# Graph attention with two GCN layers: most of the projections moved from ahead of the attention into it, and value weights of 9 columns instead of 32

## The chip, the cores and the metric

The kernel runs on one core of one Trainium2 chip. The metric is the device time of one execution in microseconds (us), the median of the runs given. PE is TensorE (matmuls), ACT is ScalarE, DVE is VectorE, POOL is GpSimd, and SP is SyncE, which issues all transfers of this kernel.

## What is computed

```python
# _layernorm: (y - mean) / sqrt(var + 1e-5) over the last axis
# N = 2708 nodes, D = 128 features, H = 8 heads; adj is 2708 x 2708, fp32
q = (x @ Wq.T).reshape(d, n, h)      # d = 128, n = 2708, h = 8
k = (x @ Wk.T).reshape(d, n, h)
v = (x @ Wv.T).reshape(d, n, h)
a = einsum('dnh,dmh->dnm', q, k) * d ** -0.5
a = softmax(a + adj + adj, axis=2)
o = einsum('dnm,dmh->dnh', a, v).reshape(n, h * d)
x = _layernorm(x + o @ Wo.T)
# second layer
h1 = adj @ (x @ W2) + b2
x = _layernorm(x + adj @ (h1 @ W4) + b4 + h1 @ res_w.T + res_b)
```

The reshape makes 128 attention batches of 2708 queries and keys with only 8 features each. One batch takes 2708 x 8 consecutive numbers of the projected rows, that is about 21 tokens of 1024 projected values.

## The kernel before

**Projections.** The first block (L300 to L349) projects all tokens: 22 chunks of up to 128 tokens (`MC`), each with the three weights. A projection is two matmuls of 128x512 into the tile `pp` (L317). For q and k, ACT writes the value rounded to the format fp32r (L326), DVE writes what the rounding left (L327) and the largest absolute value (L334, into `ends`), and SP stores both parts to DRAM (`qs`, L329; `ks`, L332). For v, ACT copies (L321) and SP stores (`vs`, L322). Amid the last chunks SP loads the keys, queries and values of the first group and the first adjacency columns. Then POOL reorders keys (`order_keys`, L252 and L256) and spreads values (`spread_values`, L268).

**Attention.** Four batches make a group (`GB`), so there are 32 groups. The queries of a group are taken in 6 blocks of 452 or 448 columns (`QBS`), the keys in 21 chunks of 128 and one of 20. A block is worked in 9 steps (`plan`), so there are 1728 steps. A step has two to four pieces and one chunk on the side (`TWO_EXP`):

- a piece is two score matmuls into one of two PSUM tiles `s` (`score`, L374), and one DVE addition of the adjacency columns to both (`add_near`, L381), into the tile `e`, of which there are four;
- the chunk on the side has three score matmuls into the PSUM tile `p`, an exponential by ACT (L456) and a product with exp of the adjacency by POOL (L457), tile `w`;
- at the end of the step one exponential by ACT (L459) over all pieces.

The matmuls of values (`add_up`, L395) sum a chunk into `acc`: four matmuls, one for each batch, each on its own 32 of the 128 output partitions. The weight of each is `v[:, m, ds(VW * j, VW)]` with `VW = 32` columns: 8 of the batch's values and 24 of ones, the first of which sums the weights. A block ends with a copy by DVE (`hand_on`, L401) and four stores (L403). In the first group ACT also makes the exponentials of the adjacency (`first_exp`, L362).

**Order.** From L407 on the order is the program's (`manual_schedule`). The generator `interleave` (L39) writes it: it keeps a model of when PE, ACT, DVE and POOL come free, with a constant for each kind of work, and picks at each point the next piece or the next `add_up` that is ready. SP's loads are put at the first piece of a step: `load_adj` keeps 8 loads ahead (`ahead`), `load_q`, `load_keys` and `load_values` are spread over a block or a group.

**The rest.** `layer0_out` divides, multiplies with Wo and normalizes; `layer1` does the two products with the adjacency. A fallback, `attention_with_maxima`, is only run where the numbers are out of range.

Of the kernel before, what the change touches and what calls it, by code (L numbers as in the profile page):

```python
# [9 lines left out]
F32 = mybir.dt.float32  # L10
F32R = mybir.dt.float32r
I32 = mybir.dt.int32
AF = mybir.ActivationFunctionType
ALU = mybir.AluOpType
AX = mybir.AxisListType
# [8 lines left out]
VW = 32  # L24
# [14 lines left out]
def interleave(plan, blocks, short, bufs=4, patience=0.1):  # L39
# [8 lines left out]
    EXP, EXP_ADDED, EXP_TILE = 0.07, 0.14, 0.37  # L48
    n_plan = len(plan)
# [12 lines left out]
    n, c, left = 0, 0, None  # L62
    while n < blocks * n_plan or queue:
        starts = []
        if n < blocks * n_plan:
# [29 lines left out]
        again = False  # L95

# [33 lines left out]
def graph_attention_gcn(ctx: ExitStack, tc: tile.TileContext, x, xT, adj, adjT, adjP, adjS,  # L130
# [35 lines left out]
    qs = dram.tile([N, 2 * H, P], F32, name="qs")  # L166
# [6 lines left out]
    ends = const.tile([P, 2, NM], F32, name="ends")  # L173
# [3 lines left out]
    with ExitStack() as s:  # L177
# [10 lines left out]
        v_short = [kept.tile([P, GB * VW], F32, name=f"v_short{i}") for i in range(2)]  # L188
        vals = [kept.tile([P, NU, GB * VW], F32, name=f"vals{i}") for i in range(2)]
        for t in k_short:  # L190
            nc.gpsimd.memset(t.bitcast(F32), 0.0)
        for t in v_short:
            nc.gpsimd.memset(t, 0.0)
            for j in range(GB):
                nc.gpsimd.memset(t[ds(32 * j, SHORT), ds(VW * j, VW)], 1.0)
        for t in vals:
            nc.gpsimd.memset(t, 1.0)
# [36 lines left out]
        def whole_tokens(r0, n):  # L234

            return ds(r0 // P, (r0 % P + n - 1) // P + 1), r0 % P

# [9 lines left out]
        def order_keys(g, i):  # L247

            t, (k, kz, _, _) = raw_keys[g], groups[g]
            if i < 8:  # L250
                n = P // 8
                nc.gpsimd.tensor_copy(k[:, :, ts(i, n)], t[:, ts(i, n * NU)].rearrange("p (q c) -> p c q", c=NU))  # L252
            else:
                for j in range(GB):
                    r = ds(32 * j, 32)
                    nc.gpsimd.tensor_copy(kz[r, ds(32 * j, SHORT)], t[r, ds(P * NU, SHORT)])  # L256

        def load_values(g, j):
# [5 lines left out]
            nc.sync.dma_start(vz[ds(32 * j, SHORT), ds(VW * j, H)], vs[ds(r0 + P * NU, SHORT), :])  # L264

        def spread_values(g, j):
            to = vals[g % 2].rearrange("p c (j e) -> p j c e", e=VW)
            nc.gpsimd.tensor_copy(to[:, j, :, :H], values[g][:, j, :].rearrange("p (c e) -> p c e", e=H))  # L268

        def load_q(g, b, js=range(GB)):  # L270

            n0, nw = QBS[b]
            if js[0] == 0:
                queries[g, b] = qpool.tile([P, P + (QB + 2 * P - 1) // P * P], F32R, tag="q", name="q")
            for j in js:
                tokens, off = whole_tokens((GB * g + j) * N + n0, nw)
                n = tokens.size
                for i in range(2):
                    to = queries[g, b][ds(32 * j + 2 * H * i, 2 * H), ds(P - off, n * P)].bitcast(F32)
                    nc.sync.dma_start(to.rearrange("p (t g) -> p t g", g=P), qs[tokens].rearrange("t r g -> r t g"))  # L280
# [17 lines left out]


        with ExitStack() as t:  # L300
            wpool = t.enter_context(tc.tile_pool(name="wqkv", bufs=1))
            sb = t.enter_context(tc.tile_pool(name="proj", bufs=4))
            ps = t.enter_context(tc.tile_pool(name="ps_proj", bufs=4, space=PSUM))

            xT_sb = wpool.tile([P, N], F32, name="xT_sb")
            nc.sync.dma_start(xT_sb[:, :P], xT[:, :P])
            w_sb = []
            for name, w in (("k", WkT), ("q", WqT), ("v", WvT)):
                w_sb.append(wpool.tile([P, H * P], F32, name=f"w{name}_sb"))
                nc.sync.dma_start(w_sb[-1], w)  # L310
            nc.sync.dma_start(xT_sb[:, P:], xT[:, P:])
            v3 = vs.rearrange("(i g) e -> i (g e)", g=P)
            for c, (i0, mi) in enumerate(MC):
                for w, dst in zip(w_sb, (ks, qs, vs)):
                    pp = ps.tile([P, 2, 512], F32, tag="pp", name="pp")
                    for h in range(2):
                        nc.tensor.matmul(pp[:mi, h, :], xT_sb[:, ds(i0, mi)], w[:, ts(h, 512)], start=True, stop=True)  # L317
                    flat = pp[:mi].rearrange("p a b -> p (a b)")
                    if dst is vs:
                        o = sb.tile([P, H * P], F32, tag="po", name="po")  # L320
                        nc.scalar.copy(o[:mi], flat)  # L321
                        nc.sync.dma_start(v3[ds(i0, mi)], o[:mi])  # L322
                    else:
                        f = half_scale if dst is qs else 1.0
                        o = sb.tile([P, 2, H * P], F32R, tag="pr", name="pr")
                        nc.scalar.mul(o[:mi, 0], flat, f)  # L326
                        nc.vector.scalar_tensor_tensor(o[:mi, 1], flat, f, o[:mi, 0].bitcast(F32), ALU.mult, ALU.subtract)  # L327
                        if dst is qs:
                            nc.sync.dma_start(dst.rearrange("i r g -> i (r g)")[ds(i0, mi)],  # L329
                                              o[:mi].bitcast(F32).rearrange("p l f -> p (l f)"))  # L330
                        else:
                            nc.sync.dma_start(dst.rearrange("r (i g) -> i r g", g=P)[ds(i0, mi)],  # L332
                                              o[:mi].bitcast(F32).rearrange("p l (e g) -> p (l e) g", g=P))
                        nc.vector.tensor_reduce(ends[:mi, int(dst is qs), c : c + 1], o[:mi, 0].bitcast(F32), AX.X,  # L334
                                                ALU.max, apply_absolute_value=True)

                if 2 <= c < 10:
                    load_keys(0, 2 * (c - 2))
                    load_keys(0, 2 * (c - 2) + 1)
                elif 10 <= c < 10 + GB:  # L340
                    load_q(0, 0, [c - 10])
                    load_values(0, c - 10)
                elif 10 + GB <= c < 10 + GB + ahead // 2:
                    load_adj(2 * (c - 10 - GB))
                    load_adj(2 * (c - 10 - GB) + 1)
            for h in range(9):
                order_keys(0, h)
            for j in range(GB):
                spread_values(0, j)  # L349

        epool = s.enter_context(tc.tile_pool(name="weights", bufs=4))
        ppool = s.enter_context(tc.tile_pool(name="products", bufs=4))
        opool = s.enter_context(tc.tile_pool(name="sums", bufs=2))
        ps = s.enter_context(tc.tile_pool(name="ps_s", bufs=2, space=PSUM))
        pq = s.enter_context(tc.tile_pool(name="ps_q", bufs=1, space=PSUM))
        pa = s.enter_context(tc.tile_pool(name="ps_a", bufs=1, space=PSUM))

# [8 lines left out]
        def score(to, g, b, m, j):  # L366
            nw = QBS[b][1]
            k, kz, _, _ = groups[g]
            q = queries[g, b][:, ds(P, nw)]
# [411 lines left out]
```

## Time and profile before

| | |
|---|---|
| median of 3 runs | 6965.26 us (6964.58 to 6968.61) |
| the profiled execution | 6968.86 us |
| its span, first to last instruction | 6967.0 us |
| mean granted PE clock | 0.994 |
| busy: PE, DVE, ACT, POOL | 97%, 88%, 94%, 81% |
| first exponential of a step (L459) starts at | 191.09 us |
| exponential of the last step ends at | 6625.1 us |
| DMA | 1654.83 MB, mean 238 GB/s |

The time of an execution is about 1.9 us longer than its span. PE's matmuls are pipelined and their ends are modelled, so PE's busy share says less than the distances from start to start. A share over the whole span mixes the projections, the attention and the rest; the stages are read one by one.

### The profile page before, as it was taken

The page shows a single profiled execution, that of the slowest core. Times are in us where ns is not written, and L with a number is a line of the kernel's source. Part 1 is how long each engine was busy: PE and PEld are TensorE (multiplying, and loading weights), DVE is VectorE, ACT ScalarE, POOL GpSimd, SP SyncE. Part 2 cuts the span into 40 slices and gives each one's busy share as a digit, 9 for nine tenths or more (in the row PEclk, how much of TensorE's full clock was granted, in tenths as well). Part 3 has the DMA queues.
Part 4 walks back from the last instruction along what each step waited for, and adds up shares of the span by engine and source line. Part 5 has one row for each costly group of instructions (what it writes and reads, how often), then busy time and mean ns, then how long its engine had stood idle before and what let it go on. Part 6 is the DMA issues. An engine that isn't in the chain of part 4 may idle for free.

```text
span 6967.0 us, 136616 instructions
## 1 busy us (share of the span) xinstructions
PE 6761.2 (97%) x50426; PEld 2168.4 (31%) x50426; DVE 6098.5 (88%) x6160; ACT 6541.9 (94%) x3659; POOL 5620.3 (81%) x2266
## 2 busy tenths in 40 slices
PE   7899999999999999999999999999999999999979
PEld 2223333333333333333333333333333333333354
DVE  5789999999999999999999999999999999999941
ACT  3999999999999999999999999999999999999920
POOL 0688888888888888888888888888888888888800
PEclk9999999999999999999999999999999999999999
DMA  9887777777777777777777777777777777777667
GB/s 340 264 247 230 235 236 243 230 233 240 234 239 228 234 244 241 229 230 237 239 239 228 234 242 241 231 227 236 238 242 229 233 243 236 235 228 237 219 199 232
DMA packets 1163854, 1654.83 MB, mean 238 GB/s; under 512 B 144372, under 2 KB 1125944, under 8 KB 1156244
## 3 DMA queue, kind: packets, MB, share of 16 engines
q1 hardware_dynamic: 1163176, 1646.00, 76.0%
q8 instruction: 399, 6.54, 0.4%
q14 instruction: 279, 2.29, 0.1%
HBM read 1563.63 MB, written 81.80 MB: 236 GB/s over the span
## 4 chain that ended last, share of the span: by engine, by line
PE 58%; ACT 12%; DVE 9%; DMA 8%; issue 7%; POOL 4%; SPq 2%; DVEq 0%; ACTq 0%; POOLq 0%
PE acc L395 29%; PE s L374 20%; DVE e L381 9%; ACT e L459 7%; ACT w L456 4%; POOL w L457 3%; PE acc L604 3%; DMA col<-in_adjP 3%; PE p L374 2%; PE acc L391 2%; DMA ecol<-ne 2%; DMA qs<-pr 1%; DMA two<-in_adjP 1%; PE s L371 1%; SPq L280 1%
## 5 line engine op out<-in xcount | busy, mean ns | idle before, releaser
L457 POOL TENSOR_TENSOR w<-w,ecol 128x1356 f32<-128x1356 f32 (+1 forms) x1728 | 5353.9, 3104 | 889.2 <-ACT w L456 731.0
L381 DVE TENSOR_TENSOR e<-s,col 128x904 f32<-128x904 f32 (+1 forms) x4608 | 4828.9, 1092 | 396.8 <-PE s L374 147.1
L459 ACT ACTIVATE e<-e 128x2712 f32<-128x2712 f32 (+5 forms) x1728 | 4729.6, 2737 | 0.8 <-DVE e L381 0.8
L395 PE MATMUL acc<-e,vals 128*32 128x452 f32 x21888 | 3812.7, 555 | 11.0 <-ACT e L459 0.5
L374 PE MATMUL s<-q,k 32*128 32x452 f32 x10944 | 2455.5, 465 | 94.7 <-DVE e L381 22.3
L456 ACT ACTIVATE w<-p 128x1356 f32<-128x1356 f32 (+1 forms) x1728 | 2417.4, 1399 | 16.0 <-DMA two<-in_adjP 13.0
L374 PEld LDWEIGHTS s<-q,k 32*128 32x128 f32 x10944 | 1023.2, 181 | 3233.4 <-DVE e L381 2737.2
L395 PE MATMUL acc<-w,vals 128*32 128x452 f32 x10368 | 1652.3, 553 | 0.0
L374 PE MATMUL p<-q,k 32*128 32x452 f32 (+1 forms) x5184 | 1261.9, 438 | 13.9 <-ACT w L456 13.6
L381 DVE TENSOR_TENSOR e<-s,two 128x904 f32<-128x904 f32 (+1 forms) x960 | 1048.4, 1092 | 160.3 <-ACT w L456 98.0
L395 PEld LDWEIGHTS acc<-e,vals 128*32 128x32 f32 x21888 | 619.3, 108 | 849.2 <-issue 781.0
L374 PEld LDWEIGHTS p<-q,k 32*128 32x128 f32 x5184 | 516.7, 182 | 37.7 <-ACT w L456 36.4
L395 PEld LDWEIGHTS acc<-w,vals 128*32 128x32 f32 x10368 | 279.1, 108 | 202.8 <-issue 178.5
L252 POOL CAST k<-k_raw 128x336 fp32r<-128x336 f32 x256 | 226.0, 884 | 16.3 <-DMA k_raw<-ks 16.3
L391 PE MATMUL acc<-e,v_short 128*128 128x452 f32 (+1 forms) x384 | 196.7, 594 | 0.0
L401 DVE COPY o<-acc 128x452 f32<-128x452 f32 x192 | 118.6, 618 | 6.2 <-PE acc L395 6.2
L326 ACT ACTIVATE pr<-pp 128x1024 fp32r<-128x1024 f32 (+1 forms) x44 | 45.1, 1024 | 79.7 <-DMA ks<-pr 44.4
L327 DVE SCALAR_TENSOR_TENSOR pr<-pp,pr 128x1024 fp32r<-128x1024 f32 (+1 forms) x44 | 53.8, 1223 | 75.3 <-ACT pr L326 70.5
L604 PE MATMUL acc<-col,xw 128*128 128x512 f32 (+2 forms) x264 | 106.0, 551 | 0.0
L496 ACT ACTIVATE sd<-mv,eps 128x1 f32<-128x1 f32 (+1 forms) x22 | 5.9, 291 | 104.7 <-DVE mv L490 104.7
L604 PE MATMUL acc<-col,hw 128*128 128x512 f32 (+2 forms) x264 | 104.1, 545 | 0.0
L616 ACT COPY hw<-ph 128x128 f32<-128x128 f32 (+1 forms) x22 | 5.4, 266 | 98.7 <-PE ph L615 98.6
(77 smaller groups left out, 979.9 us busy)
## 6 DMA issues: line engine op xcount, KB each, us to landing
col<-in_adjP SPq DMA_DIRECT2D x1965, 226.0 KB
two<-in_adjP SPq DMA_DIRECT2D x1440, 226.0 KB
ecol<-ne SPq DMA_DIRECT2D x1395, 226.0 KB
col<-in_adjP SPq DMA_DIRECT2D x393, 224.0 KB
two<-in_adjP SPq DMA_DIRECT2D x288, 224.0 KB
ecol<-ne SPq DMA_DIRECT2D x279, 224.0 KB
col<-in_adjT SPq DMA_DIRECT2D x210, 256.0 KB
k_raw<-ks SPq DMA_DIRECT2D x512, 84.6 KB
```

Source lines behind the costliest of these rows:

```text
L252: nc.gpsimd.tensor_copy(k[:, :, ts(i, n)], t[:, ts(i, n * NU)].rearrange("p (q c) -> p c q", c=NU))
L280: nc.sync.dma_start(to.rearrange("p (t g) -> p t g", g=P), qs[tokens].rearrange("t r g -> r t g"))
L371: nc.tensor.matmul(to[:, :nw], kz, q, start=True, stop=True)
L374: nc.tensor.matmul(to[:, :nw], k[r, m, :], q[r], start=True, stop=True)
L381: nc.vector.tensor_add(e[:, ds(at, 2), :nw], st[:, :, :nw], a)
L391: nc.tensor.matmul(a[:, :nw], vz, e[:, t, :nw], start=False, stop=False)
L395: nc.tensor.matmul(a[ds(32 * j, VW), :nw], v[:, m, ds(VW * j, VW)], e[:, t, :nw], start=(m == first_chunk), stop=(m == last_chunk))
L401: nc.vector.tensor_copy(o[:, :nw], acc.pop((g, b))[:, :nw])
L456: nc.scalar.activation(w[:, :, :nw], sp[:, :, :nw], AF.Exp, scale=2.0)
L457: nc.gpsimd.tensor_mul(w[:, :, :nw], w[:, :, :nw], exp_cols[g, b, two][:, :nw].unsqueeze(1).to_broadcast([P, 3, nw]))
L459: nc.scalar.activation(e[:, :at, :nw], e[:, :at, :nw], AF.Exp, scale=2.0)
L604: nc.tensor.matmul(acc[:, :nw], src[:mw, m, :], t[:mw, :nw], start=(m == 0), stop=(last is None and m == NM - 1))
```

## The change

The projections of the first two chunks of tokens (`FIRST = 2`, 256 tokens, enough for the first three groups) stay ahead of the attention, and the pools that only they used are gone: they borrow the tiles `w`, `e` and `s`. The reordering of the first group's keys is shared out to POOL, DVE and ACT. The other 20 chunks are projected half a projection at a time: 120 halves, each one matmul 128x512 into a tile `s`. The planner puts one ahead of steps 2, 8, ... 50, and then one ahead of every 13th step from 56 to 1486. DVE alone does the work after the matmul: three operations for q and k, one copy for v. SP loads the half's weight again (256 KB) right after the half before, and stores the result at the second piece of the following step.

The values of a batch take 9 columns (`VW = H + 1`) instead of 32. The first chunk of a block, which starts the sum, still uses 32, from a small tile `v_first` of its own, that `spread_values` also fills. `qs` is laid out as `ks` is, by feature row, so that a query load takes 16 rows of up to 1808 bytes each.

```diff
-VW = 32
+VW = H + 1
...
-def interleave(plan, blocks, short, bufs=4, patience=0.1):
+def interleave(plan, blocks, short, amid=(), bufs=4, patience=0.1):
...
+    PROJECT, SPLIT = 0.95, 1.75
...
-        if n < blocks * n_plan:
+        if n in amid and c == 0 and seen < n:
+            starts.append((added[-2] + HOP, "amid"))
+        elif n < blocks * n_plan:
...
+        if what == "amid":
+            pe += PROJECT
+            added.append(max(added[-1], pe + SHOWN) + SPLIT)
+            seen = n
+            yield "amid", n, None, None
+            continue
...
-    qs = dram.tile([N, 2 * H, P], F32, name="qs")
+    qs = dram.tile([2 * H, R], F32, name="qs")
...
-            nc.gpsimd.tensor_copy(to[:, j, :, :H], values[g][:, j, :].rearrange("p (c e) -> p c e", e=H))
+            v = values[g][:, j, :].rearrange("p (c e) -> p c e", e=H)
+            nc.gpsimd.tensor_copy(to[:, j, :, :H], v)
+            nc.gpsimd.tensor_copy(v_first[g % 2][:, ds(32 * j, H)], v[:, first_chunk, :])
...
+            q = queries[g, b] = qpool.tile([P, QB], F32R, tag="q", name="q")
+            for j in range(GB):
                 for i in range(2):
...
+                    nc.sync.dma_start(q[ds(32 * j + 2 * H * i, 2 * H), :nw].bitcast(F32),
+                                      qs[:, ds((GB * g + j) * N + n0, nw)])
...
+        proj = s.enter_context(tc.tile_pool(name="proj", bufs=2))
...
+        def split(o, src, i, end, mul=nc.vector.tensor_scalar_mul):
+
+            f = half_scale if i == 1 else 1.0
+            mul(o[:, 0].bitcast(F32R), src, f)
+            nc.vector.scalar_tensor_tensor(o[:, 1].bitcast(F32R), src, f, o[:, 0], ALU.mult, ALU.subtract)
+            nc.vector.tensor_reduce(end, o[:, 0], AX.X, ALU.max, apply_absolute_value=True)
+
+        def load_half(n):
+            c, i, h = halves[n]
+            i0, mi = MC[c]
+            if i == h == 0:
+                given[c] = proj.tile([P, P], F32, tag="xc", name="xc")
+                nc.sync.dma_start(given[c][:, :mi], xT[:, ds(i0, mi)])
+            given[c, i, h] = proj.tile([P, NB], F32, tag="wc", name="wc")
+            nc.sync.dma_start(given[c, i, h], projections[i][0][:, ts(h, NB)])
+
+        def project(n):
+
+            c, i, h = halves[n]
+            i0, mi = MC[c]
+            dst = projections[i][1]
+            pp = ps.tile([P, 2, NB], F32, tag="s", name="s")
+            nc.tensor.matmul(pp[:mi, 0, :], given[c][:, :mi], given.pop((c, i, h)), start=True, stop=True)
+            o = proj.tile([P, 2, NB], F32, tag="pr", name="pr")
+            if i == 2:
+                nc.vector.tensor_copy(o[:mi, 0], pp[:mi, 0])
+                return lambda: nc.sync.dma_start(dst.rearrange("(i g) e -> i (g e)", g=P)[ds(i0, mi), ts(h, NB)], o[:mi, 0])
+            split(o[:mi], pp[:mi, 0], i, ends[:mi, i, ds(2 * c + h, 1)])
+
+            def store():
+                for l in range(2):
+                    nc.sync.dma_start(dst.rearrange("r (i g) -> i r g", g=P)[ds(i0, mi), ds(H * l + 4 * h, 4)],
+                                      o[:mi, l].rearrange("p (e g) -> p e g", g=P))
+            return store
...
+        for n in range(ahead):
+            load_adj(n)
+        load_half(0)
+        for i, (_, dst) in enumerate(projections):
+            for c in range(FIRST):
+                pp = ps.tile([P, 2, NB], F32, tag="s", name="s")
+                for h in range(2):
+                    nc.tensor.matmul(pp[:, h, :], first_x[:, ts(c, P)], first_w[:, ts(2 * i + h, NB)], start=True, stop=True)
...
+            if i == 1:
+                for h in range(16):
+                    load_keys(0, h)
+                load_q(0, 0)
...
+        for h in range(9):
+            order_keys(0, h, (nc.gpsimd.tensor_copy, nc.vector.tensor_copy, nc.scalar.copy)[h % 3])
...
-                nc.tensor.matmul(a[ds(32 * j, VW), :nw], v[:, m, ds(VW * j, VW)], e[:, t, :nw],
-                                 start=(m == first_chunk), stop=(m == last_chunk))
+                if m == first_chunk:
+                    nc.tensor.matmul(a[ds(32 * j, 32), :nw], v_first[g % 2][:, ds(32 * j, 32)], e[:, t, :nw],
+                                     start=True, stop=False)
+                else:
+                    nc.tensor.matmul(a[ds(32 * j, VW), :nw], v[:, m, ds(VW * j, VW)], e[:, t, :nw],
+                                     start=False, stop=(m == last_chunk))
...
+        amid = list(range(2, 54, 6))
+        amid += range(56, 56 + 13 * (len(halves) - len(amid)), 13)
...
+            if what == "amid":
+                at = amid.index(n)
+                stores.append(project(at))
+                if at + 1 < len(halves):
+                    load_half(at + 1)
+                continue
...
+            if c == 1 and stores:
+                stores.pop()()
```

## The prediction

> **What bounds the kernel now.** I read the stages first: the busy time by stretches, whose columns are the stretch, then busy us and instructions of each engine, the clock granted to PE, the DMA share and GB/s.
>
> ```profile
> 0.00:187.00 187.00, 129.49 (x270) 49.41 (x270) 103.08 (x89) 68.88 (x68) 15.57 (x37) 0.92 1.01 336
> 187.00:225.00 38.00, 34.44 (x211) 10.93 (x215) 31.75 (x31) 34.52 (x25) 24.81 (x8) 0.83 0.83 254
> 1000.00:6000.00 5000.00, 4932.57 (x38212) 1515.39 (x38204) 4591.92 (x4496) 4999.40 (x2698) 4378.53 (x1749) 1.00 0.76 236
> 6600.00:6967.00 367.00, 322.00 (x1418) 181.43 (x1410) 129.34 (x333) 65.80 (x96) 22.51 (x13) 0.96 0.68 212
> ```
>
> The first stage is all 22 chunks of projections: the DMA share is 1.01 and no compute engine is full, so transfers end it. The middle stage is another regime: ACT is busy 4999.4 of 5000 us. The next view, ACT's timeline (start, duration), tells whether that is work or stretched waiting.
>
> ```profile
> 2011.54 1.38 ACT L456 ACTIVATE w<-p 128x1344 f32<-128x1344 f32 x1
> 2012.73 3.27 ACT L459 ACTIVATE e<-e 128x3584 f32<-128x3584 f32 x1
> 2015.81 1.37 ACT L456 ACTIVATE w<-p 128x1344 f32<-128x1344 f32 x1
> ```
>
> 1344 elements take 1.19 us from start to start, 3584 take 3.08: the difference is 0.84 ns an element, the same everywhere. ACT works without a pause; only fewer elements could shorten this stage, and the change leaves ACT's exponentials alone. ACT's waits from 225 to 6600 us say the same:
>
> ```profile
> ACT w L456 <- PE p L374: 1.2, 3, 0.6
> ACT w L456 <- PE s L374: 0.4, 1, 0.4
> ```
>
> But the reserve behind it is small. I took, from the timeline of DVE and ACT, the lead with which the last addition (L381) of a step ends before the step's exponential (L459) starts. It is the same in nearly every block of nine steps (step 0 to 8): 0.32, 2.01, 0.67, 1.19, 1.21, 0.33, 0.86, 0.20, 1.11 us. 0.20 is the least ever seen, so at step 7 ACT is just waiting, and from 0 and 5 it is 0.1 away. That wait is hidden in the overlap of two activations, and shows only in start-to-start: 65 ns more at step 6's end and 14 ns at step 7 than elsewhere, 0.08 us a block.
>
> PE's timeline shows its spacing (all from one stretch):
>
> ```profile
> 2010.04 0.96 PE L395 MATMUL acc<-e,vals 128*32 128x448 f32 x8
> 2010.93 0.47 PE L374 MATMUL s<-q,k 32*128 32x448 f32 x2
> 2011.34 0.56 PE L395 MATMUL acc<-e,vals 128*32 128x448 f32 x1
> 2011.74 0.54 PE L395 MATMUL acc<-e,vals 128*32 128x448 f32 x1
> 2012.23 0.82 PE L374 MATMUL s<-q,k 32*128 32x448 f32 x4
> ```
>
> Four batches' value products run side by side, in two passes: 11.34, 11.74, next work at 12.23. PE goes from cluster to cluster with few gaps: against the usual minimum of each kind of transition I find some 225 us of slack in 5000, 1.5 us a block of 33.4.
>
> **What the Trainium skill says.** "TensorE: Matmul & The Clock Gate", section "LDWEIGHTS": a load's time goes with the number of columns, P/1.2 ns, not with rows. The trace agrees: at 452 columns pass to pass is 403 ns, 27 above the 376 that the shortest transitions take, and 32/1.2 is 27. By the same page 9 columns cost 7.5 ns (an estimate; the trace has no such load). "ScalarE: Activation LUTs", section "What ACT_TABLE_LOAD costs": 0.833 ns an element; the trace's 0.84 agrees. "VectorE: DVE Perf Modes", section "Mode 1× (REGULAR)": fp32 and PSUM operands fall back to one element a cycle, at 0.96 GHz; the 904 elements of L381 in 1.09 us agree.
>
> **The change, part by part.** *Start.* In before the first exponential of a step (L459) starts at 191.09 us. After, the chain is: wk in at 5.3 (as now); k for two chunks through PE, ACT (1.02) and DVE (1.22 + 1.21 each): stores of ks at 11 and 14; q follows as banks come free: stores at 16 and 18. The queue ahead of them holds 1.7 MB of x and weights, 2.5 MB of adjacency, 0.3 MB of the next half; with the four 1 MB stores 8.5 MB, at 336 GB/s 25 us, so q has landed at about 28. SP issues 16 key loads and 8 query loads at 0.4 us from 19 on: landed at about 35. Then 9 key reorderings on three engines (POOL 0.88 each): 38. Queries land meanwhile. Four additions of 1.0 us: **first exponential at 44 us** (36 if the transfers overlap better, 55 if each hop waits for its store; the value stores and loads come after, and are needed a step or two later). Removed: 191 − 44 = **147 us** (136 to 155).
>
> *Nine value columns.* 20 of the 21 chunks (the first stays 32 wide) save 27 − 7.5 ns ahead of both passes, 0.04 us a chunk, 0.78 us of PE a block. On ACT's path that is worth only the 0.08 us a block that it waits now: 192 × 0.08 = 15, I take **−10 us**. Its use is slack.
>
> *Projections amid.* 120 halves: 9 in the first 54 steps, then 111, one every 13 steps (48 us) up to step 1486. Each has a 128x512 matmul, 2 × 0.43 (the spacing of L317) plus a load: 0.95 us of PE; at 0.69 a block this is 0.66 us, less than the 0.78 gained, and within the slack of 1.5 anyhow. A k or q half (80 of them) gives DVE three operations of 512 elements, (1.22 − 0.53) − 0.08 overlap = 0.6 us each: 1.8 us. A v half gives 0.6. DVE's own work is 29 additions at 1.01 and one copy, 29.8 of 33.4 us; 1.0 more fits on average. On ACT: nothing. What counts is the moment: DVE is 1.8 us late at once, and ACT's lead is 0.1 to 1.8 above its minimum. I walked the nine steps (13 steps apart, the halves fall on each in turn): DVE's pauses beyond back-to-back, that can be used to catch up, are 0.28, 0.66, 0.56, 0, 0.49, 0.37, 0.65, 0.25, 0.35 us in steps 0 to 8. Late time less pauses less lead is what ACT loses: inserted ahead of step 0 to 8 1.4, 0.1, 0.8, 0.8, 0.8, 1.3, 0.9, 1.6, 1.1, mean 0.97. The shorter loads raise the leads by some 85 ns a step (2.2 chunks × 0.04), 0.2 until the weak step comes: 0.75 us. 73 such halves: **+55**. For 38 v halves the rule gives 0.07, but PE's 0.95 against a score pair's 0.4 comes on top: 0.3, **+11**. In the first 54 steps ACT has a further 0.55 us a step (L362) and leads of 0.8 and more: **+2** for all nine.
>
> *Queues.* SP gets a weight load (256 KB) and one or two stores per half; the stores wait for DVE's split. Behind them wait the next steps' adjacency loads, issued 8 loads, over two steps, ahead; SP already waits for DVE once a block and ACT never sees it:
>
> ```profile
> SPq L403 <- DVE o L401: 856.9, 150, 9.0
> ```
>
> That is 5.7 us a time. I cost this at nothing; were the cover gone, a load late by 1 us 111 times would be 111. DMA: 86 MB more in the middle less the 512-byte query packets (2.9% of the engines' time before, fetched as 1808-byte rows after): from 76% to about 80%. POOL gets four copies of 8 columns a group, under 0.4 us in 200: nothing, POOL pauses 12% of the time.
>
> *Sum:* −147 − 10 + 55 + 11 + 2 = −89. 6967.0 − 89 = 6878 span, + 1.9 around it (6968.86 profiled), − 3.6 since the median, 6965.26, is that much below the profiled execution: **6876 us**.
>
> **Rivals.** (1) *Everything hides*: shorter loads raise the leads so far that a split costs 0.2 us. Start −150, relief −15, stalls 15: 6815. For it: DVE has 2.6 us unused a block even with the halves. Against: steps 5 and 7 have four additions, 4.1 us of a 4.3 us step. (2) *PE becomes the bound*: loads of nine columns cost as much as 32 (they may have been covered otherwise) and each half's 0.95 us is exposed: 111 × 0.95 = 105, and 2: 6925. (3) *The start stays long*: store, load, reorder and value round trip wait one for the other, first exponential near 90: 6922. (4) **Slower**: every half empties the pipeline. The half takes one of only two PSUM banks of the scores; PE stops behind it until DVE has split it, DVE stops until PE has scored again, so that 0.95 + 1.8 us reach ACT at step ends: 2.75 × 73 + 1.55 × 38 = 260, 7070. It decides from a mean of 1.3 us a half, 147/111. Against: PE has value products to do meanwhile, and DVE's 0.36 us a step of pauses take part of it. (That nine columns stop the four products from running side by side would be dearer still; nothing in the trace speaks for it.)
>
> **How the numbers follow.** Forecast 0.60, (1) 0.15, (2) 0.08, (3) 0.06, (4) 0.11. The forecast's own bounds: stall 0.4 to 1.2 us a half of k or q, start 136 to 155: 6840 to 6925. With rivals (1) to (3) the range is 6815 to 6945. Faster by over 0.2% (the limit of what a measurement of this kernel can tell), under 6951: 0.85; within 0.05, where stalls of 1.2 to 1.5 us meet a start of 136; slower 0.10.
>
> **What would show it.** First step's exponential near 44 us, DMA share no longer 1 for 187 us; value products 384 ns pass to pass; ACT still above 98% busy between 225 and 6600, its pauses in front of L459's successor lying at the steps after a half, of 0.5 to 1.5 us, one per 13 steps; a stretch without halves (after step 1486, about the last 900 us) at 33.3 us a block. Wrong if ACT pauses longer than 1.5 us per half, if it waits for DMA, or if value products are spaced as before.

## The result, and the profile after

The changed kernel is slower by half a per cent: **7000.66 us**, median of 5 runs (6991.54 to 7009.01), beside 6964.81 for the kernel before, a ratio of 1.0052 (95% interval 1.0037 to 1.0066). The profiled execution took 7000.04 us, its span 6998.3.

I compared four instants of the two traces, in us:

| | before | after | change in the stretch |
|---|---|---|---|
| first exponential of a step starts | 191.1 | 47.7 | −143.4 |
| exponential of step 54 starts | 418.2 | 281.9 | +7.0 |
| exponential of the last step ends | 6625.1 | 6656.5 | +167.8 |
| end of the span | 6967.0 | 6998.3 | −0.2 |

So the start gains what was forecast, and the attention gives it all back and 31 us more. The stretches of the kernel after say the same (columns as before: stretch, then busy us and instructions of PE, PEld, DVE, ACT, POOL, then PE's granted clock, the DMA share and GB/s).

```profile
0.00:44.00 44.00, 14.60 (x30) 5.49 (x30) 12.40 (x12) 10.32 (x14) 7.37 (x26) 0.79 0.80 252
44.00:82.00 38.00, 35.49 (x213) 10.27 (x215) 33.46 (x35) 35.12 (x25) 26.64 (x16) 0.88 0.91 278
1000.00:5000.00 4000.00, 3881.43 (x29767) 1127.52 (x29764) 3680.13 (x3673) 3892.99 (x2091) 3401.95 (x1432) 0.99 0.78 241
5850.00:6600.00 750.00, 738.85 (x5741) 214.46 (x5733) 689.76 (x676) 750.00 (x405) 652.40 (x265) 1.00 0.74 230
6600.00:6998.00 398.00, 353.33 (x1656) 191.26 (x1652) 157.82 (x361) 97.22 (x113) 48.49 (x21) 0.96 0.68 214
```

ACT, which was idle 0.5 us of these 4000 in before, is now idle 107 of them. In the stretch without halves (from 5850) it is busy to the last hundredth again, 33.3 us a block. So it is the halves. In the views of waits, a line names who waited, for whom, the us in total, how often and the longest. ACT's waits from 225 to 6600 us, where before had two lines with 1.6 us:

```profile
ACT e L512 <- DVE e L417: 57.1, 82, 1.1
ACT w L509 <- PE p L410: 49.0, 85, 1.3
ACT w L509 <- PE s L410: 22.7, 22, 2.6
ACT w L509 <- POOL w L510: 14.5, 16, 1.0
```

ACT waits for PE (two lines, 107 times) more often than for DVE (82 times); the forecast had only DVE late, but for a small share in the v halves. These waits leave out what two overlapping activations hide, so in what follows **loss** is another sum: from ACT's timeline in the profiled execution, the start-to-start distances of its exponentials, less the distance that the same two forms keep where nothing waits. From step 54 to the last half it is 182.8 us, against 15.1 in before: 1.65 us for each of the 111 halves, 1.80 for k, 1.71 for q and 1.44 for v.

What the prediction said of the nine columns' own time is so. The value weights load faster, 89 ns against 108 in before, and passes of value products follow each other after 384 ns (403 before), as 9 columns give by the Trainium skill, "TensorE: Matmul & The Clock Gate", section "LDWEIGHTS". In the groups of the page, with busy us and mean ns:

```profile
L435 PEld LDWEIGHTS acc<-e,vals 128*9 128x9 f32 x20352 | 457.1, 89 | 818.4 <-issue 794.5
```

SP now also waits for DVE at the halves' stores (L358), and a little less at the stores of a block (L443; 696.1 us in before), and no wait of ACT names a DMA. SP's waits, 1000 to 5000 us:

```profile
SPq L443 <- DVE o L441: 574.2, 116, 9.0
...
SPq L358 <- DVE pr L330: 73.9, 22, 6.8
```

### The profile page after: what moved, and what is told of

The parts are those of the page before. It is cut to its first block, busy times and chain, and to the rows that moved or that the text cites. A ratio compares the mean times of both kernels' runs of the same rounds, so it can differ in the third digit from the quotient of the medians.

```text
span 6998.3 us, 137155 instructions
## 1 busy us (share of the span) xinstructions
PE 6733.7 (96%) x50426; PEld 2044.4 (29%) x50426; DVE 6186.2 (88%) x6363; ACT 6509.2 (93%) x3605; POOL 5624.8 (80%) x2387
## 4 chain that ended last, share of the span: by engine, by line
PE 49%; DMA 14%; DVE 12%; issue 8%; ACT 7%; SPq 5%; POOL 5%; DVEq 0%; ACTq 0%; POOLq 0%
PE acc L435 23%; PE s L410 16%; DVE e L417 10%; DMA col<-in_adjP 6%; POOL w L510 5%; ACT w L509 3%; ACT e L512 3%; PE acc L657 3%; DMA two<-in_adjP 3%; SPq L286 3%; DMA ecol<-ne 2%; PE p L410 2%; PE acc L427 2%; PE acc L432 1%; PE s L349 1%
## 5 line engine op out<-in xcount | busy, mean ns | idle before, releaser
L512 ACT ACTIVATE e<-e 128x2712 f32<-128x2712 f32 (+5 forms) x1728 | 4625.9, 2677 | 61.1 <-DVE e L417 60.2
L435 PE MATMUL acc<-e,vals 128*9 128x452 f32 x20352 | 3564.6, 547 | 0.5 <-ACT e L512 0.2
L410 PE MATMUL s<-q,k 32*128 32x452 f32 x10944 | 2488.0, 464 | 134.8 <-DVE e L417 71.2
L509 ACT ACTIVATE w<-p 128x1356 f32<-128x1356 f32 (+1 forms) x1728 | 2312.3, 1338 | 94.4 <-PE p L410 54.2
L435 PE MATMUL acc<-w,vals 128*9 128x452 f32 x10368 | 1634.3, 548 | 0.0
L410 PE MATMUL p<-q,k 32*128 32x452 f32 (+1 forms) x5184 | 1282.5, 444 | 21.9 <-ACT w L509 20.9
L435 PEld LDWEIGHTS acc<-e,vals 128*9 128x9 f32 x20352 | 457.1, 89 | 818.4 <-issue 794.5
L435 PEld LDWEIGHTS acc<-w,vals 128*9 128x9 f32 x10368 | 207.6, 89 | 217.4 <-issue 184.4
L432 PE MATMUL acc<-e,v_first 128*32 128x452 f32 (+1 forms) x1536 | 188.3, 559 | 52.5 <-DVE o L441 46.3
L349 PE MATMUL s<-wc,xc 128*128 128x512 f32 (+1 forms) x240 | 134.2, 641 | 0.0
```

The lines of the kernel that those rows point to most:

```text
L349: nc.tensor.matmul(pp[:mi, 0, :], given[c][:, :mi], given.pop((c, i, h)), start=True, stop=True)
L410: nc.tensor.matmul(to[:, :nw], k[r, m, :], q[r], start=True, stop=True)
L432: nc.tensor.matmul(a[ds(32 * j, 32), :nw], v_first[g % 2][:, ds(32 * j, 32)], e[:, t, :nw], start=True, stop=False)
L435: nc.tensor.matmul(a[ds(32 * j, VW), :nw], v[:, m, ds(VW * j, VW)], e[:, t, :nw], start=False, stop=(m == last_chunk))
L509: nc.scalar.activation(w[:, :, :nw], sp[:, :, :nw], AF.Exp, scale=2.0)
L512: nc.scalar.activation(e[:, :at, :nw], e[:, :at, :nw], AF.Exp, scale=2.0)
```

## The experiments

Median and ratio stand against the kernel before on the same chip, whose medians were 6964.65 to 6965.82 us. All kernels keep the changed start unless it is said otherwise.

### Nine columns by themselves

`nine_only` is the kernel before with the nine columns and nothing else.

```diff
-VW = 32
+VW = H + 1
+        v_first = [kept.tile([P, P], F32, name=f"v_first{i}") for i in range(2)]
+                if m == first_chunk:
+                    nc.tensor.matmul(a[ds(32 * j, 32), :nw], v_first[g % 2][:, ds(32 * j, 32)], e[:, t, :nw], ...)
```

> The kernel before with nothing changed but the value weights: 9 columns, the first chunk of a block still 32. By the prediction 0.78 us of PE a block is saved, but only the 0.08 us that ACT waits in a block can be had: 6950 to 6960. If PE and not ACT were the bound of the attention, 192 x 0.78 = 150 us less, 6815.

Measured: 6964.26 us, 0.9998 (0.9989 to 1.0007): nothing. The leads of the additions did not rise by 85 ns a step either: step 7's is still 0.20 us, steps 0 and 5 still have 0.32 and 0.27. So the 0.78 us of PE's time a block did not reach the weak steps. I take it that an addition's moment is set there by the written order and by when its buffers come free, and that the time became pauses of PE elsewhere. The trace shows a part of it: PE's waits for DVE and ACT from 225 to 6600 us are 58.8 us, against 24.5 in before.

`after_32_columns` is the changed kernel with 32 columns: `VW = 32`.

> The changed kernel with value weights of 32 columns again, the first chunk as now from its own tile. By the prediction the nine columns free 0.78 us of PE a block, which the halves (0.66 a block) use up: without them 160 blocks lack up to 0.66 us each, 7060 to 7120. Rival (ACT's lead is set by the order and by the buffers, not by PE's mean load, as nine columns alone gained nothing): 6995 to 7030.

Measured: 7026.75 us, 1.0086 (1.0069 to 1.0103), loss 205.7 against 182.8. Amid the halves the nine columns are worth 26 us. They pay here, where PE is short of time at the halves, and not without halves.

### A half taken apart, in the changed kernel's order

`x_order` takes the matmul and DVE's work out of each half, `x_pe` only DVE's. In `x_dve` DVE does operations of the same count and size on the loaded weights, without matmul or PSUM tile.

```diff
 # x_order; x_pe keeps the first two lines
-            pp = ps.tile([P, 2, NB], F32, tag="s", name="s")
-            nc.tensor.matmul(pp[:mi, 0, :], given[c][:, :mi], given.pop((c, i, h)), start=True, stop=True)
-            o = proj.tile([P, 2, NB], F32, tag="pr", name="pr")
+            o = zeros
-                nc.vector.tensor_copy(o[:mi, 0], pp[:mi, 0])
-            split(o[:mi], pp[:mi, 0], i, ends[:mi, i, ds(2 * c + h, 1)])
 # x_dve, for k and q
+            nc.vector.scalar_tensor_tensor(o[:mi, 0].bitcast(F32R), src, 1.0, src, ALU.mult, ALU.max)
+            nc.vector.scalar_tensor_tensor(o[:mi, 1].bitcast(F32R), src, 1.0, o[:mi, 0], ALU.mult, ALU.subtract)
```

> The changed kernel with the 120 halves emptied: the planner still reserves their place, and SP still loads the weights and stores (a tile of zeros), but a half has no matmul and no DVE work. It leaves out all projections but the first two chunks. Baseline of the reckoning: before less the 143 us that the first exponential moved ahead and less the 15 us that ACT waited in it, some 6810. Theory order (the order that the planner writes around a half, with 1.75 us reserved for DVE, is what makes ACT wait): most of the loss of 175 us stays, 6930 or more. Theories PE (its 0.95 us a half is what is late) and DVE (its split is late): 6810 to 6840. Theory DMA (loads and stores of the halves delay the adjacency): also 6900 or more, but then with DVE or POOL waiting for transfers.

> As the changed kernel, but DVE does nothing for a half: the matmul goes into its bank, which is free at once, and zeros are stored. It leaves out the results of all but two chunks of projections. Theory PE: 0.95 us of each of the 111 later halves comes through, the emptied kernel plus 80 to 105 us. Theory DVE: within 20 us of the emptied kernel. Theory order: within 20 us of the emptied kernel, and both near 7000.

> As the changed kernel, but with no matmul in a half: DVE does its three operations (one for v) on the loaded weights in SBUF instead, and no PSUM bank is taken. It leaves out the results of all but two chunks of projections. Theory DVE, by the walk of the prediction with 0.97 us a half of k or q: the emptied kernel plus 70 us. Theories PE and order: within 20 us of the emptied kernel.

Measured: `x_order` **6927.17** us (0.9944, 0.9927 to 0.996), loss 107.9; `x_pe` **6990.38** (1.0035, 1.0022 to 1.0047), loss 165.1; the whole 7000.66. The first is the surprise: halves that are empty on every compute engine still cost ACT about 1 us each, whatever their kind (0.98, 1.01, 0.93). Some 19 us of this loss fall in stretches in which PE was granted half its clock, mostly at the halves ahead of step 5 (last section). The matmul adds 63 us, and DVE's 280 operations only 10, which is little more than the scatter of single executions (6991.54 to 7009.01 beside 6984.85 to 6995.74).

`x_dve` took 7286.11 us (1.0458) and doesn't answer its question. Its operations were no stand-in. Tile `pr` in its trace, then in the changed kernel's (ns min/median/max, first and last start):

```profile
L354 DVE SCALAR_TENSOR_TENSOR pr<-wc,pr x80: 680/1256/3826, 54.1 to 5945.9; 128x512 fp32r<-128x512 f32 x76, 20x512 fp32r<-20x512 f32 x4
```

```profile
L331 DVE SCALAR_TENSOR_TENSOR pr<-s,pr x80: 678/692/696, 51.6 to 5657.1; 128x512 fp32r<-128x512 f32 x76, 20x512 fp32r<-20x512 f32 x4
```

The same operation with both inputs in SBUF took up to 3.8 us, with one in PSUM 0.69. The Trainium skill, "SBUF — State Buffer", section "Who interferes with whom", says that such an instruction contends with a GpSimd instruction that reads SBUF; POOL's product (L511 in this kernel, about 3.1 us long) is running most of the time here. The trace agrees, and shows how. From 225 us on, 144 of these operations on 128 rows (L351, L353, L354) started while a product was running, and 140 of them ended 0.54 to 0.57 us after that product ended. The 23 of L354 that met no product took 0.69 us. So such an operation waits here for the end of the product. In this run PE was granted half its clock for 495 us between 225 and 6600 us.

### What the planner is told of a half

`interleave` counts 0.95 us of PE (`PROJECT`) and 1.75 us of DVE (`SPLIT`) for every half and writes the order by that. `plan_none` counts nothing, `plan_by_kind` counts less, and least for v.

```diff
-    PROJECT, SPLIT = 0.95, 1.75
+    PROJECT, SPLIT = 0.0, 0.0                    # plan_none
+    PROJECT, SPLIT = 0.95, (1.3, 1.3, 0.55)      # plan_by_kind
-            added.append(max(added[-1], pe + SHOWN) + SPLIT)
+            added.append(max(added[-1], pe + SHOWN) + SPLIT[kind[n]])
```

> The changed kernel with its halves whole, but the planner counts a half as nothing (PROJECT and SPLIT 0), so that the order of score pairs and value products around it stays as if there were none. Theory order: the 117 us that the emptied kernel lost go, and PE's and DVE's share (63 and 10 us) stays: about 6880. Rival: the reserve is needed, since PE now stands at the second score pair until DVE has freed the bank of the half, some 1.3 us for each of 73 halves of k and q: 7000 or more. Theory DMA: 7000, as before.

> The changed kernel, but the planner reserves what the bank is held in the trace: 1.3 us for k and q (two operations of 0.69), 0.55 for v, instead of 1.75 for each. Theory order: the v halves (1.44 us each now) lose about half of it, those of k and q a quarter: 6945. Rival (the reserve doesn't matter, PE's 0.95 does): 6990 to 7005.

Measured: 6974.16 us (1.0013, 1.0006 to 1.002) and 6975.44 (1.0014, 1.0007 to 1.0021), 26 and 25 us less than the changed kernel. Two things are in this gain. With the right size for v, a v half's loss falls from 1.44 to 0.84 us. And the half clock is all but gone (one and no stretch of it, against 13), which is worth some 17 to 20 us (last section); the loss of a k or q half is not smaller in `plan_by_kind` where the clock was full. Why a v half gains, the changed kernel's timeline shows around a v half ahead of step 459 (start us, duration, engine):

```profile
1828.54 1.02 PE L349 MATMUL s<-wc,xc 128*128 128x512 f32 x2
...
1829.49 0.48 PE L410 MATMUL s<-q,k 32*128 32x452 f32 x2
1829.60 0.69 DVE L352 COPY pr<-s 128x512 f32<-128x512 f32 x1 [0.57 <-PE s L349]
...
1830.21 1.09 DVE L417 TENSOR_TENSOR e<-s,col 128x904 f32<-128x904 f32 x1
...
1830.66 0.94 PE L435 MATMUL acc<-e,vals 128*9 128x452 f32 x8
...
1831.53 0.47 PE L410 MATMUL s<-q,k 32*128 32x452 f32 x2
...
1832.08 1.10 DVE L417 TENSOR_TENSOR e<-s,col 128x904 f32<-128x904 f32 x1 [0.78 <-PE s L410]
...
1833.42 1.30 ACT L509 ACTIVATE w<-p 128x1356 f32<-128x1356 f32 x1 [0.61 <-PE p L410]
```

The copy frees the half's PSUM tile at 1830.29. The planner took it to be held 1.75 us, so it had value products written ahead of the second score pair, and PE works through them until 1831.53. PE is busy throughout; yet DVE, which ended its first addition at 1831.30, stands 0.78 us, and ACT 0.61.

`x_empty_none` and `x_pe_none` repeat `x_order` and `x_pe` with `PROJECT, SPLIT = 0.0, 0.0`.

> The emptied halves (no matmul, no DVE work, loads and stores as in the changed kernel, zeros stored; the projections of all but two chunks are left out) with a planner that counts a half as nothing. If the 117 us that the emptied kernel lost came from the order alone: 6965 less 143 of the start, 6810 to 6830. If they came from the loads and stores: 6900 or more, as with the planner's reserve.

> The same with the matmul of each half put back (no DVE work, the bank is free at once; results left out). Theory PE time: a half's 0.95 us reaches ACT whatever the order: 0.5 to 0.95 us a half, 60 to 105 us above the kernel without it, 6875 to 6925, and the 50 to 100 left to 6974 are DVE's holding of the bank. Rival (the holding of the bank is all): within 20 us of the kernel without it.

Measured: 6868.74 us (0.9861, loss 54.0) and 6952.44 (0.9981, loss 134.9). Without a reserve, the kernel with empty halves takes 58 us less than with it; the matmul again costs 84, and DVE's part now 22 (to 6974.16).

### The order left as it was

In `frozen` the planner isn't told of halves at all: it writes before's order to the letter, and a half is put in at the first piece of its step. `x_empty_frozen` and `x_pe_frozen` are `x_order` and `x_pe` with this edit.

```diff
-        for what, n, c, beside in interleave(plan, len(steps) // len(plan), NU, amid):
-            if what == "amid":
+        for what, n, c, beside in interleave(plan, len(steps) // len(plan), NU):
+            if what == "piece" and c == 0 and n in amid:
                 at = amid.index(n)
                 stores.append(project(at))
```

> Emptied halves (loads and stores alone, zeros stored, the projections of all but two chunks left out), and the planner is not told of them at all: score pairs and value products stand in the very order of the kernel before, the halves' transfers at the same steps. If the loss of the emptied kernels (6927 with the planner's reserve, 6869 with a reserve of nothing) is order: 6810 to 6825, all of the start's 143 us won. If loads and stores cost: 6850 or more.

> The order of the kernel before, and each half's matmul slipped in ahead of its step (no DVE work, results left out). Theory PE time: PE is late by 0.95 us and more, ACT's lead at the weak steps is 0.1: 0.7 to 1.0 us a half, 80 to 110 us above the emptied kernel of this order, about 6910. Rival (PE's slack takes it): within 30 us of the emptied kernel.

> The changed kernel whole, results kept, but in the order of the kernel before. If order and PE time make up the loss: the kernel without DVE work in this order plus 10 to 25 us, about 6930, 70 below the changed kernel. If the planner's reserve does some good (value products while DVE holds the bank): 6975 or more.

Measured: **6830.84** us (0.9811, 0.9794 to 0.9827), **6896.58** (0.9906, 0.9889 to 0.9922) and **7018.12** (1.0083, 1.0066 to 1.01). The first has all the transfers of the halves, and its loss is 13.4 us, that of before; its profiled execution, 6822.80 us, has the whole gain of the start. So loads and stores cost nothing, even at a DMA share of 0.81. Its stretch from 1000 to 5000 us, and what is left of ACT's waits in the attention (the lines left out belong to the work after it):

```profile
1000.00:5000.00 4000.00, 3934.80 (x30565) 1138.86 (x30557) 3673.78 (x3597) 3998.88 (x2158) 3510.18 (x1479) 1.00 0.81 248
```

```profile
...
ACT w L507 <- PE p L409: 0.7, 1, 0.7
ACT e L510 <- DVE e L416: 0.4, 1, 0.4
```

The matmul alone raises the loss to 78.6, by 0.59 us a half: most of its 0.95 us comes out at ACT. The half also takes its turn at the two tiles `s`, which could delay the next score pair by itself. It is PE's time that ends last, though. In `x_pe_frozen` that pair starts 0.95 us or more after the half (median 1.06), and in 94 of 113 cases over 0.2 us after DVE had freed the pair's own tile. DVE's part costs 122 us here. The timelines of PE and DVE at the same k half, ahead of step 576, in `x_pe_frozen` and then in `frozen`:

```profile
2231.40 1.02 PE L351 MATMUL s<-wc,xc 128*128 128x512 f32 x2
...
2232.35 0.67 PE L410 MATMUL s<-q,k 32*128 32x452 f32 x4
```

```profile
2277.59 1.02 PE L349 MATMUL s<-wc,xc 128*128 128x512 f32 x2
...
2278.54 0.47 PE L410 MATMUL s<-q,k 32*128 32x452 f32 x2
2278.65 0.69 DVE L330 TENSOR_SCALAR pr<-s 128x512 fp32r<-128x512 f32 x1 [0.57 <-PE s L349]
...
2279.38 0.69 DVE L331 SCALAR_TENSOR_TENSOR pr<-s,pr 128x512 fp32r<-128x512 f32 x1
...
2280.12 0.54 PE L410 MATMUL s<-q,k 32*128 32x452 f32 x2 [1.10 <-DVE pr L331]
...
2280.58 1.09 DVE L417 TENSOR_TENSOR e<-s,col 128x904 f32<-128x904 f32 x1
```

Without DVE's work the next two score pairs go out together. With it, the second pair needs the PSUM tile that the half holds until DVE's second operation ends, and PE, with value products behind that pair in its order, stands 1.10 us. (The view counts this wait in 67 of the k and q halves.) PE's waits in `frozen`, 225 to 6600 us:

```profile
PE s L410 <- DVE pr L331: 65.8, 67, 1.1
PE s L410 <- DVE e L417: 51.6, 245, 1.0
PE s L410 <- DVE pr L352: 7.1, 21, 0.4
```

Behind L331 (k and q) and L352 (v) PE stands 73 us, of the 122. By the loss, DVE's part is about 1.5 us for a k or q half, and 0.2 for a v half, which gives its tile back after 0.69 us. Here too the half clock has a share: `frozen` has nine stretches of it, each beginning 4 to 5 us after a k or q half starts, right behind such a wait; where the clock was full, DVE's part is 1.2 to 1.3 us a k or q half.

`frozen_late_max` tests DVE's own lateness: the third operation, which reads no PSUM, goes behind the first addition of the step.

```diff
             split(o[:mi], pp[:mi, 0], i, end, late=True)      # without the tensor_reduce
             def store():
+                nc.vector.tensor_reduce(end, o[:mi, 0], AX.X, ALU.max, apply_absolute_value=True)
```

> The whole kernel in the order of the kernel before (7018), with DVE's third operation of a k or q half (the largest absolute value, 0.67 us, which reads SBUF alone) moved behind the first addition of the following step. If ACT loses what the first additions of the step are late by: up to 0.67 us for each of 73 halves, 50 us less, 6970. If it is the bank that PE waits for, which the first two operations free: within 15 us of 7018.

Measured: 6999.69 us (1.0049, 1.0033 to 1.0066), 18 us less than `frozen`. Taking 0.68 us of DVE's work from ahead of the addition is worth 0.25 us a half at most. In the profiled executions even this is the half clock: a k and a q half at full clock lose 1.93 and 2.00 us in `frozen`, and 1.92 and 1.98 here, where six stretches at half clock are left of nine. So the lateness of the third operation costs nothing that shows. I didn't separate the rest of the 122 between the held tile and the first two operations any further.

The medians together, in us, with the step that each column adds:

| order written for | halves empty | + matmul | + DVE's work |
|---|---|---|---|
| no halves (before's order) | 6830.84 | 6896.58 (+66) | 7018.12 (+122) |
| halves that cost nothing | 6868.74 | 6952.44 (+84) | 6974.16 (+22) |
| 0.95 and 1.75 us each (the change) | 6927.17 | 6990.38 (+63) | 7000.66 (+10) |

The planner's reserve does what it is for: DVE's part falls from 122 to 10 us. But the order that avoids this costs 96 by itself (6927.17 less 6830.84). PE's part is there in every row. The half clock is inside these numbers: some 19 us of the 96, and some 17 of the 122.

### Where a half stands

In the changed kernel's order, the loss of a k or q half ahead of step 0 to 8 of a block is 2.25, 0.79, 0.96, 0.84, 1.21, 3.48, 2.19, 2.48 and 1.27 us. At step 5 it is 2.09 where the clock was full, and 3.95 in the nine of twelve cases with a stretch of half clock. A period of 13 visits all nine steps. `row1` puts every half ahead of step 1 (one in each block, so that the last stands ahead of step 1054); `row1_plan_none`, `row1_by_kind` and `row1_frozen` add the edits above.

```diff
-        amid += range(56, 56 + 13 * (len(halves) - len(amid)), 13)
+        amid += range(64, 64 + 9 * (len(halves) - len(amid)), 9)
```

> The changed kernel with the 111 later halves every 9 steps, from step 64, always ahead of step 1 of a block, where the trace of the changed kernel shows 0.55 to 0.85 us of ACT's waiting a half, instead of every 13 steps, where the mean over the nine places is 1.65. Theory lead (what a half costs is set by the lead of the steps that follow): 111 x 0.9 = 100 us less, 6900. Rival (ACT must lose what PE lacks on average, wherever the half is): with one half in each block instead of one in 1.44 blocks PE has too little slack, 7000 or more.

> Both of the above: halves ahead of step 1 of each block from step 64, and a planner that counts them as nothing. If the order and the place each cost by itself: 6840 to 6880. If the place alone removes what the order costs: as the halves ahead of step 1 alone.

> Halves ahead of step 1 of each block, and a planner that reserves 1.3 us for k and q and 0.55 for v. If a reserve of the true length is better than none, less than the 6928 of the planner that counts nothing; if any reserve pushes score pairs back, between 6928 and 6966, nearer to 6928 by the v halves.

> Whole halves, ahead of step 1 of each block from step 64 on, in the order of the kernel before: the two things that helped most, together. By the sums so far 6895 to 6925; as good as the planner that counts nothing (6928) if the order is no longer what costs there.

| | us | ratio (95%) | loss: all, and per k, q, v half |
|---|---|---|---|
| `row1` | 6966.22 | 1.0001 (0.9993 to 1.001) | 142.7; 1.37, 1.30, 1.19 |
| `row1_by_kind` | 6957.38 | 0.9987 (0.998 to 0.9994) | 135.6; 1.47, 1.44, 0.78 |
| `row1_frozen` | 6968.08 | 1.0006 (0.9997 to 1.0014) | 147.7; 1.64, 1.65, 0.72 |
| `row1_plan_none` | **6927.66** | **0.9947 (0.993 to 0.9963)** | 108.2; 1.17, 1.18, 0.59 |

Place alone gains 34 us of the changed kernel's time, less than the 0.79 us of step 1 had promised, and part of it is the half clock's (4 stretches against 13). In `row1` the loss is again nearly the same for each kind, so it is not DVE's operations that make it. In before's order (`row1_frozen`) the place gains 50 us on `frozen`, but the k and q halves still lose 1.64 us, and the sum stays above the 6895 to 6925 us that I had expected. With nothing counted, `row1_plan_none` is the fastest whole version that I found, 38 us below before and 73 below the changed kernel. Its waits of ACT and of PE, 225 to 6600 us:

```profile
ACT w L509 <- PE p L410: 48.0, 106, 0.7
...
ACT e L512 <- DVE e L417: 2.6, 16, 0.2
```

```profile
PE s L410 <- DVE pr L331: 17.1, 74, 0.3
```

PE's wait for the half's tile is 0.3 us at most, against 1.1 in `frozen`: in this order the value products of one chunk (8 matmuls, 0.88 us from start to start) stand right behind a half. ACT now waits for PE alone, 0.45 us a half.

`row1_none_late_max` adds the late third operation to it.

> The best version so far (halves ahead of step 1 of each block, a planner that counts them as nothing, 6928), with the same move of the largest absolute value. If DVE's lateness at the first addition is what is left of the k and q halves' loss (1.17 us against 0.59 for v): up to 45 us less, 6885 to 6905. If it is the bank: 6920 to 6935.

Measured: 6929.08 us (0.9947, 0.9931 to 0.9964): no different. Here the third operation's time does not reach ACT. How the 108 us that are left divide between PE's matmul and the order, I didn't run at this place.

## Why the prediction was wrong

The forecast was 6876 us, with 6815 to 6945 as the range; 7000.66 is 125 above it and on the other side of no change. Two steps failed: PE's 0.95 us a half, taken to lie "within the slack of 1.5 anyhow", cost 63 us, and the new order of the matmuls, which the sum has no term for, cost 96. Rows 1 and 3 of the table above split the miss:

| term | predicted | measured | from |
|---|---|---|---|
| start, nine columns, first steps, transfers | 6810 (6876 less 66 for the halves' stalls) | 6830.8 | `x_empty_frozen` |
| another order | 0, not costed | +96 | `x_order` less `x_empty_frozen` |
| PE's 0.95 us a half | +8 (in the v halves' +11) | +63 | `x_pe` less `x_order` |
| DVE's lateness | +58 | +10 | whole less `x_pe` |

- **Start: right.** −147 was forecast for the first exponential and −143.4 came; the DMA share fell to 0.80 in the first 44 us, and nothing speaks for rival (3). The first 54 steps cost 7.0 us, where +2 was forecast. Of the 21 us in the first row, 8 are the distance of this kernel's median from its profiled execution, and 10 those of the nine columns, which follow.
- **Nine columns: right in size, wrong in effect.** 384 ns came as forecast. The steps "−10 us" and "raise the leads by some 85 ns a step" failed: `nine_only` gains nothing and raises no weak lead. (Nor is 0.20 us "the least ever seen" at step 7: two of 178 blocks of before have 0.09 and 0.16.) I had taken a mean saving of PE for an earlier score at the weak step.
- **PE: the step that failed most plainly.** "0.66 us, less than the 0.78 gained, and within the slack of 1.5 anyhow" compares means over a block; only the v halves were given anything for it. Slack in other steps of the block did not help the step that the half is in. 60 to 80% of the 0.95 us reach ACT, in all three orders (63 to 84 us over 111 halves). That is the mechanism of rival (2), and its 105 us was the better size; but it took the nine columns to bring nothing for another reason, and left out the order.
- **DVE: the wrong reason.** "0.75 us" a k or q half was worked out from DVE's lateness. In the order that I worked it out in, before's, it is 1.5 (1.2 to 1.3 at full clock): a half holds a PSUM tile until DVE's second operation ends, and PE stands up to 1.1 us behind it. I had this in rival (4) and set it aside because PE has "value products to do meanwhile". In before's order they stand behind the waiting score pair, and PE keeps to its order.
- **The order: never costed.** The diff hands the halves to the planner, with 1.75 us for every one, v too. The prediction walked before's nine steps as if they stayed. The rewritten order puts value products ahead of score pairs, which frees PE from the wait (+10 in place of +122) and makes the pair late instead (+96, of which some 19 are the half clock). What stands between a half and the next score pair is fixed before the kernel runs, so it could have been read from the new order; I didn't read it.
- **Rival (4)** had the right place and sign, and the point from which it decides, 1.3 us a half; measured is a loss of 1.65. Its own size, 2.34 on average, was too large, and not "0.95 + 1.8 us" reach ACT, but part of the 0.95 and an order. 0.11 was too little for "slower", which it alone of the rivals stood for.
- **Queues and DMA: right.** SP's wait for DVE at a store reaches 6.8 us; yet no wait of ACT names a transfer, and the transfers alone cost nothing (`x_empty_frozen`). POOL is named in 16 of ACT's waits, 14.5 us in all; what made it late there I didn't follow.
- **The tail and the stretch without halves: right**, 33.3 us a block. Pauses "of 0.5 to 1.5 us" a half were too short: at step 5 a k or q half lost 3.48.

## What to carry to other kernels

Where one engine is busy 99.9% and the next 97%, as here, slack is a matter of places, not of means: before an operation is called hidden, find in the timeline what stands directly behind it on its engine and whether that is what the full engine waits for. In before's order an extra user of a double-buffered PSUM tile held PE until its last reader ended, so PE needs independent work written right behind it, and only as much as that reader takes. Where a planner writes the order, a change of its costs is a change of the kernel: run it once with the new work empty, to have the order's price apart. And look at the clock granted in the same stretches: here PE's pauses went ahead of stretches at half clock, which cost further time.

## What the runs showed of the hardware

- **DVE beside POOL.** DVE's two-input operation on 512 elements has a median of 1.26 us and up to 3.83 with both inputs in SBUF while POOL multiplies, and 0.69 with one input in PSUM. Of 144 that started during a product of POOL, 140 ended 0.54 to 0.57 us after the product's end (`x_dve`).
- **Half clock.** Between 411 and 6500 us the changed kernel's PE was granted half its clock 13 times, 61 us in all, for 3.4 or 6.8 us at a time (before: once); `x_order` had 14, `frozen` 9, `plan_none` one, `row1_plan_none` and `plan_by_kind` none. The Trainium skill, "TensorE: Matmul & The Clock Gate", section "What's actually happening", puts the half clock after an idle window of about 3.4 us. In the matmul records of this trace no gap is longer than 1.2 us. But the 3.41 us before each of the 13 are always a stretch in which PE was little busy: 2.1 to 2.3 us in twelve, 2.7 in one, where the mean is 3.3. One of them, and the half clock behind it (columns as before):

```profile
1783.71:1787.12 3.41, 2.12 (x19) 0.87 (x19) 3.28 (x4) 3.41 (x2) 1.70 (x1) 1.00 1.06 307
1787.12:1790.53 3.41, 3.41 (x18) 0.41 (x10) 2.50 (x3) 2.95 (x2) 2.73 (x1) 0.50 1.12 360
```

  I cut the time at full clock into such stretches, 1765 of them; the 13 are among the 47 with the least work of PE. `plan_by_kind`, `row1_plan_none`, `nine_only` and `x_pe_frozen`, in which no stretch has less than 2.7 us of work, have no half clock between 411 and 6500 us; the single one of before follows its least busy stretch, 2.8 us. So what goes ahead of the half clock here is several short pauses of PE, and an idle window of 3.4 us is not needed: where page and trace differ, the trace decides. Not every such stretch is followed by it, and what else decides isn't shown. Nine of the 13 come 10 to 12 us after a k or q half ahead of step 5, and there its price can be read: such a half lost 2.0 to 2.2 us without it, 3.0 to 3.8 with one of 3.4 us, and 4.2 to 4.6 with one of 6.8. In all, some 17 to 20 us of the changed kernel's loss of 182.8 come with the half clock.
